# Transfers of the image preparation spread over twelve steps, and activation tables loaded in steps of their own

## The chip, the core and the metric

The kernel runs on one core of a Trainium2 chip. The metric is the device time of one execution in microseconds; the figure for a kernel is the median of several runs. The engines of the core run side by side, each through its own list of instructions in order: TensorE (PE in the profile, with its weight loads as PEld), VectorE (DVE), ScalarE (ACT), GpSimd (POOL) and SyncE (SP), which here does little but issue transfers (DMAs). They wait for each other by semaphores.

## What is computed

Four layers work on an image x of 4 batches, 32x32 pixels and 16 channels, each of the form x + layer(group_norm(x)). Layers 0, 1 and 3 are the heavy ones: every output pixel has a 3x3 convolution kernel of its own, whose result over the whole image is compared with the image and summed with weights. Layer 2 is a small dynamic program with two steps of sums, a sigmoid and a maximum. Cut to what matters:

```
def conv_layer(inputs, M, W, G):           # layers 0, 1 and 3 (inputs are normalized)
    first   = einsum('ijyx,byxc->bijc', M, inputs)
    kern    = transpose(G, (0, 1, 5, 4, 2, 3)).reshape(h * w * f, c, 3, 3)
    shifted = conv(x_nchw, kern, 'SAME')   # one 3x3 kernel per output pixel and channel
    diff    = relu(inputs[:, None, None] - shifted)
    second  = einsum('ijyx,bijyxc->bijc', W, diff)
    return first - second

def dp_step(f, r, W, b):                   # layer 2, twice
    g = sigmoid(ft[:, :, :, None, :] + rt[:, None, :, :, :] + b)
    return max(g, axis=2)

def _gn(v):                                # before every layer
    return (g - mean) / sqrt(var + eps)    # over 8 groups of channels
```

## The kernel before

**Phases and steps.** The batches are taken in two groups g of two. A phase is one heavy layer for one group; there are six, in the order (group 0, layer 0), (1, 0), (0, 1), (1, 1), (0, 2), (1, 2), where layer 2 in this count is the reference's layer 3. A phase has eight chunks of 128 output pixels, and a chunk 32 steps, one for each output channel and batch. A step fills one pair of PSUM banks (tile pc) with the convolution result for 128 output pixels against 1024 image pixels. There are 256 steps in a phase and 1536 in all, which this text numbers from 0.

In a step, `conv_layer` does this, in order: `first_part` issues eight matmuls of TensorE (L584, weights WU and WL against images iy and iz) and ScalarE's scaling of the result (L614); `second_part` of the step before issues six more matmuls (the weights WD and W9 against iyz and im9, into the scaled tile) and VectorE's weighted sum of the negative part (L630, tile junk). So TensorE needs L614 of a step one step later.

**Preparation of weights.** Four output channels (eight steps) form a unit. `prep_parts` prepares a unit's weights two units ahead, in eight pieces, one per step, which this text letters A to H: A, VectorE cuts off the upper bits (L191); B, ScalarE halves W9 (L167); C, ScalarE L224 and GpSimd L225 and L226; D, ScalarE L228 and GpSimd L229; E, GpSimd subtracts columns of the identity from the next unit's raw weights (L202); F, nothing; G, SP issues two transfers that copy parts with its halves exchanged (L235, 384 KB each), and the load of raw weights two units on (L107, 768 KB); H, nothing. The copy of a unit is seven steps ahead of its first use. Each piece tells with its yield whether the step is IDLE, that is, whether ScalarE has no such work in it: A, E, F, G and H are.

**Work behind the steps.** All else is written as generators (`behind`), which are resumed after a step's own instructions. They yield a number (so many steps until they go on) or IDLE (go on in the next idle step). In every phase but the last, `before_conv` prepares the images for the next one. `group_norm` takes sums on VectorE, with several small reductions `gap` steps apart (`totals`, used for the mean and then for the variance), the root on ScalarE (L324, then DVE's reciprocal L326 and the product on POOL L327). Then VectorE transposes the normalized image (L341), SP writes it to DRAM as xs with four transfers (L346), and two steps later SP begins the 24 transfers that read it back shifted, one for each of 12 (slot, row, tap) and each half h (L356, 68 KB each). They go out six per step over four steps, and after a pause of 24 or 12 steps the image tiles are made from raw (`split`, L259 and L263, `halve` and `difference`). As phase 0 takes its images directly, there are five such preparations, for phases 1 to 5.

Before layer 2, `interval_layer` runs behind phases 3 and 4. Its `step` does a DP step: eight times POOL adds a table (L541) and VectorE takes a maximum (L548), six steps apart; then ScalarE takes the sigmoid (L552), and SP writes the result back with four transfers.

**Activation tables.** ScalarE evaluates the root and the sigmoid from tables of which one set is held at a time; copies and scalings work with either. The program loads a set (ACT_TABLE_LOAD) ahead of an instruction that needs another than the last. It does so for the root at the start (L786), for the first sigmoid of each interval layer (L552), and for the next root after it (L324): five loads.

**Queue of SP.** L107, L113 (512 KB of the weights of the sum, once in a chunk), L235, L346 and L356 are all issued by SP, in program order, each after its own waits. Eight semaphores serve these transfers in turn, so each also waits until the eighth before it has landed.

Of the kernel before, what the change touches and what calls it, by code (L numbers as in the profile page):

```python
# [8 lines left out]
F32 = mybir.dt.float32  # L9
F32R = mybir.dt.float32r  # L10
I32 = mybir.dt.int32
AF = mybir.ActivationFunctionType
# [25 lines left out]
QI = H // NQ  # L38
# [3 lines left out]
def net_kernel(ctx: ExitStack, tc: tile.TileContext, x, xq, xi, convs, iv_w, iv_b, out):  # L42
# [26 lines left out]
    nc = tc.nc  # L69
    ctx.enter_context(tc.manual_schedule())  # L70

    const = ctx.enter_context(tc.tile_pool(name="const", bufs=1))
# [22 lines left out]
    IDLE = 0  # L95
# [49 lines left out]
    load_plain(nc.sync, 1, 0, FU)  # L145


    eps = const.tile([P, 1], F32, name="eps")
    nc.vector.memset(eps, 1e-5)
    ident = const.tile([P, P], F32, name="ident")  # L150
# [15 lines left out]
    def halve(dst, src, mask):  # L166
        nc.scalar.activation(dst, src, AF.Copy, scale=mask[:, 1:2])  # L167

    def halve_rest(dst, src, mask):
        nc.vector.scalar_tensor_tensor(  # L170
            dst, src, mask[:, 0:1], dst.bitcast(F32), op0=ALU.mult, op1=ALU.add
        )
# [11 lines left out]
    def image(v, x):  # L184
        return v.rearrange("... (y x) -> ... y x", x=x)[..., :H]
# [68 lines left out]
    def split(eng, g, b, name, pause=IDLE):  # L254

        high = upper(image(raw[:, :2, b], HP), 2, f"x{name}{b}")
        yield 1
        for s in range(2):
            eng.tensor_tensor(  # L259
                image(iz[g][:, s, b], H), image(raw[:, s, b], HP), image(high[:, s], H), ALU.subtract  # L260
            )
            yield pause
            nc.scalar.activation(iy[g][:, s, b], high[:, s], AF.Copy, scale=EPS)  # L263

    def difference(eng, g, b, s):
        eng.tensor_tensor(
            iyz[g][:, s, b], iy[g].bitcast(F32)[:, s, b], iz[g].bitcast(F32)[:, s, b],
            ALU.subtract,
        )
# [4 lines left out]
    def spread(stat):  # L274
        return stat.unsqueeze(1).unsqueeze(3).to_broadcast([P, NT, GC // 2, 2])

    def pair_view(ap):
        return ap.rearrange("p t (g s) -> p t g s", s=2)

    def group_norm(g, name, dst, gap):  # L280


        def sums(src):
            nc.vector.tensor_reduce(
                part[:, : GC // 2], src.rearrange("p t (g s) -> p g t s", s=2), axis=AX.XY, op=ALU.add
            )

        def totals(name):

            turned = work.tile([P, 32], F32, tag="turned", name=f"turned_{name}")  # L290
            nc.vector.transpose(turned, part)
            by_quarter = work.tile([32, 4], F32, tag="by_quarter", name=f"by_quarter_{name}")
            for q in range(4):
                nc.vector.tensor_reduce(
                    by_quarter[:, q : q + 1], turned[32 * q : 32 * q + 32], axis=AX.X, op=ALU.add
                )
            yield gap
            total = work.tile([P, 32], F32, tag="total", name=f"total_{name}")
            for q in range(4):
                nc.vector.tensor_reduce(  # L300
                    total[32 * q : 32 * q + 32, 0:1], by_quarter, axis=AX.X, op=ALU.add
                )
            yield gap
            whole = work.tile([P, 32], F32, tag="whole", name=f"whole_{name}")
            nc.vector.transpose(whole, total[:, 0:1].to_broadcast([P, 32]))
            return whole[:, : GC // 2]

        sums(X[g])
        yield gap
        m = yield from totals(f"m{name}")  # L310
        mean = work.tile([P, GC // 2], F32, tag="mean", name=f"mean_{name}")
        nc.gpsimd.tensor_scalar_mul(mean, m, 1.0 / (2 * NP))
        xc = work.tile([P, NT, GC], F32, tag="xc", name=f"xc_{name}")
        nc.gpsimd.tensor_tensor(pair_view(xc), pair_view(X[g]), spread(mean), ALU.subtract)
        sq = work.tile([P, NT, GC], F32, tag="sq", name=f"sq_{name}")
        nc.gpsimd.tensor_tensor(sq, xc, xc, ALU.mult)
        yield 4
        sums(sq)
        yield gap
        v = yield from totals(f"v{name}")  # L320
        yield 2
        yield IDLE
        rstd = work.tile([P, GC // 2], F32, tag="rstd", name=f"rstd_{name}")
        nc.scalar.activation(rstd, v, AF.Sqrt, bias=eps, scale=1.0 / (2 * NP))  # L324
        yield 2
        nc.vector.reciprocal(rstd, rstd)  # L326
        nc.gpsimd.tensor_tensor(pair_view(dst), pair_view(xc), spread(rstd), ALU.mult)  # L327
        yield 3
# [5 lines left out]
    def before_conv(g, layer):  # L334
        xn = work.tile([P, NT, GC], F32, tag="xn", bufs=2, name=f"xn_{g}_{layer}")
        xns[g] = xn
        yield from group_norm(g, f"c{g}{layer}", xn, 1 if layer == 2 else 4)

        nc.vector.transpose(  # L341
            xt[g][:, :, 1 : 1 + H], xn
        )
        inner = xs[g][:, HP : HP + H * HP].rearrange("p (t r n) -> p r t n", r=ROWS, n=HP)
        for r in range(ROWS):
            nc.sync.dma_start(inner[:, r], xt[g][GC * r : GC * (r + 1)])  # L346
        yield 2
        xsv = xs[g].rearrange("(b c) n -> c b n", b=GB)
        at = 0
        for slot, row, tap in [(tap // 4, tap % 4, tap) for tap in range(8)] + [  # L350
            (2, row, 8) for row in range(4)
        ]:
            for h in range(2):
                off = (HI * h + tap // 3) * HP + tap % 3
                r0 = 64 * h + C * row
                nc.sync.dma_start(  # L356
                    raw[r0 : r0 + C, slot ^ h if slot < 2 else 2, :, :RUN], xsv[:, :, off : off + RUN]
                )
            at += 1
            if at % 3 == 0:  # L360
                yield 1
        yield 12 if layer == 2 else 24
        for b in range(GB):
            yield from split(nc.gpsimd, g, b, f"{g}{layer}")
            yield IDLE
            halve(image(im9[g][:, b], H), image(raw[:, 2, b], HP), low_x)
            for s in range(2):
                difference(nc.gpsimd, g, b, s)
            yield 3
            halve_rest(image(im9[g][:, b], H), image(raw[:, 2, b], HP), low_x)  # L370
            yield 1
# [73 lines left out]
    def interval_layer(g):  # L445
# [85 lines left out]
        def step(name, ftp, bias):  # L531

            ft = ivp.tile([P, QI, T1], F32, tag="ft", name=f"ft_{name}{g}")
            nc.scalar.copy(ft, ftp)
            yield 2
            s = ivp.tile([P, QI, T1], F32, tag="s", name=f"s_{name}{g}")
            last = None
            for i in range(QI + 1):
                if i < QI:
                    t = dp[i % 2]  # L540
                    nc.gpsimd.tensor_tensor(  # L541
                        t,
                        ft[:, i, :].unsqueeze(1).to_broadcast([P, T1, T1]),
                        rt,
                        ALU.add,
                    )
                if last is not None:
                    nc.vector.tensor_reduce(s[:, i - 1, :], last, axis=AX.X, op=ALU.max)  # L548
                last = t
                yield 6  # L550
            yield IDLE
            nc.scalar.activation(s, s, AF.Sigmoid, bias=bias)  # L552
            for q in range(NQ):
                nc.sync.dma_start(r[R:, QI * q : QI * (q + 1), :], s[GC * q : GC * (q + 1)])
            yield 4
# [125 lines left out]
    def behind(phase):  # L681
        g, layer = phases[phase]
        if phase == 0:
            yield from rest_of_start()
            nc.scalar.dma_start(X[1], x[1])
            zeros(1)
            yield 1
            yield from constants()
        if phase + 1 < len(phases):
            g1, layer1 = phases[phase + 1]  # L690
            if layer1 == 2:
                yield from interval_layer(g1)
            terms = g1 == NG - 1 and layer1 < NL - 1
            if terms:
                mt = load_first_terms(layer1)
            yield from before_conv(g1, layer1)
            if terms:
                yield from first_terms(layer1, mt)
        if phase == len(phases) - 1:
            mt = load_first_terms(layer)  # L700
            yield 24
            yield from first_terms(layer, mt)
            yield 4
            nc.sync.dma_start(out[1 - g], X[1 - g])
# [228 lines left out]
```

## Time and profile before

| | us |
|---|---|
| median of 3 runs | 2594.79 (2590.87 to 2596.59) |
| the profiled execution | 2596.11 |
| its span in the profile | 2594.4 |
| L630 on VectorE, 1536 times | 1879.3 busy, 1224 ns each |
| L614 on ScalarE, 1520 times | 1531.8 busy, 1008 ns each |
| L225, L226, L229 on POOL, 190 times each | 246 to 247 busy each, about 1300 ns each |
| ACT_TABLE_LOAD, 5 times | 1283 ns each |
| L107, L235, L356 to landing, median | 7.2, 5.0, 2.4 |

The span is the time from the first to the last instruction of the profiled execution; the device time has 1.7 us more. Busy times are of the engine named, and engines overlap. A line of the timeline gives the start, the duration, the engine, the line, the operation, the tiles and how many instructions were merged; in brackets is the engine's idle time ahead of it. SPq is the sequencer of SP, where issuing a transfer takes its time. In the list of waits a line reads: who waited, for whom, the sum, how often and the longest.

### The profile page before, as it was taken

Reading aid. Unit: us, or ns where it says so; the run is one execution under the profiler, and the core shown is the slowest. Engines: PE = TensorE matmul, PEld = TensorE weight load, DVE = VectorE, ACT = ScalarE, POOL = GpSimd, SP = SyncE. Lnnn points to the kernel's source line nnn. Section 1 sums busy time; section 2 is a strip of 40 time slices with the busy share of each in tenths; the row PEclk is TensorE's granted clock in tenths of the full one; section 3 lists DMA queues with packets and bytes.
Section 4 is the critical chain, followed back from the end, with each engine's and each line's share of the span. In section 5 each row is a group of like instructions: output and inputs, shape, how many; then the busy total and the mean of one; then the engine's idle time right before and its main releaser. Section 6 shows DMA issues by size and latency. Waiting matters only on the chain.

```text
span 2594.4 us, 56655 instructions
## 1 busy us (share of the span) xinstructions
PE 2564.2 (99%) x21906; PEld 2158.5 (83%) x21906; DVE 2084.0 (80%) x3620; ACT 1893.7 (73%) x2169; POOL 1101.9 (42%) x990
## 2 busy tenths in 40 slices
PE   8999999999999999999999999999999999999999
PEld 5998888889888888888888887798888779788887
DVE  8887777878777877777788878788888878777777
ACT  4777677777777767777777777677777777677776
POOL 3444333444333435333345554354646344333332
PEclk9999999999999999999999999999999999999999
DMA  5655444464444653444444444544444466444442
GB/s 168 186 143 154 121 131 137 119 165 127 130 137 129 193 151 110 137 130 130 131 139 131 131 123 132 153 131 120 125 131 135 130 150 193 119 139 131 130 131 52
DMA packets 81182, 353.80 MB, mean 136 GB/s; under 512 B 18448, under 2 KB 20368, under 8 KB 80144
## 3 DMA queue, kind: packets, MB, share of 16 engines
q1 hardware_dynamic: 79920, 349.57, 48.1%
q8 instruction: 172, 2.82, 0.5%
q14 instruction: 98, 0.80, 0.1%
q10 hardware_dynamic: 864, 0.58, 0.1%
q0 software_dynamic: 128, 0.02, 0.0%
HBM read 199.19 MB, written 0.98 MB: 77 GB/s over the span
## 4 chain that ended last, share of the span: by engine, by line
PE 94%; DMA 2%; issue 1%; SPq 1%; DVE 0%; ACT 0%; POOL 0%; ACTq 0%; DVEq 0%; POOLq 0%
PE pc L584 93%; DMA parts<-parts 1%; PE pf L386 1%; SPq L356 1%; DMA raw<-in_g 0%; DMA raw<-in_xi 0%; ACT pc L614 0%; DVE junk L630 0%; DMA first<-in_g 0%; POOL parts L225 0%; PE ps_l L509 0%; SPq L346 0%; POOL W L226 0%; SPq L235 0%; PE ps_r L522 0%
## 5 line engine op out<-in xcount | busy, mean ns | idle before, releaser
L630 DVE SCALAR_TENSOR_TENSOR junk<-pc,WT 128x1024 f32<-128x1024 f32 x1536 | 1879.3, 1224 | 485.5 <-PE pc L584 440.1
L614 ACT ACTIVATE pc<-pc 128x1024 f32<-128x1024 f32 x1520 | 1531.8, 1008 | 665.1 <-PE pc L584 640.1
L584 PE MATMUL pc<-iy,parts 64*128 64x512 f32 x6080 | 1074.4, 394 | 13.5 <-DMA parts<-parts 13.5
L584 PE MATMUL pc<-iyz,parts 64*128 64x512 f32 x6080 | 1070.8, 394 | 4.0 <-ACT pc L614 4.0
L584 PE MATMUL pc<-iz,parts 64*128 64x512 f32 x6080 | 1070.6, 393 | 0.0
L584 PEld LDWEIGHTS pc<-iy,parts 64*128 64x128 f32 x6080 | 681.0, 185 | 129.0 <-DMA parts<-parts 17.0
L584 PEld LDWEIGHTS pc<-iz,parts 64*128 64x128 f32 x6080 | 681.5, 185 | 109.3
L584 PEld LDWEIGHTS pc<-iyz,parts 64*128 64x128 f32 x6080 | 660.3, 185 | 100.1 <-ACT pc L614 3.9
L584 PE MATMUL pc<-im,W 64*128 64x512 f32 x3072 | 725.4, 397 | 0.0
L225 POOL TENSOR_TENSOR parts<-raw,upper_w 128x512 fp32r<-128x512 f32 x190 | 246.1, 1295 | 1065.9 <-PE pc L584 923.7
L584 PEld LDWEIGHTS pc<-im,W 64*128 64x128 f32 x3072 | 382.7, 185 | 57.9 <-issue 3.4
L226 POOL TENSOR_TENSOR W<-W,raw 128x512 fp32r<-128x512 f32 x190 | 246.7, 1298 | 4.6 <-ACT W L167 4.6
L229 POOL TENSOR_TENSOR parts<-parts 128x512 fp32r<-128x512 f32 x190 | 246.7, 1298 | 2.0 <-ACT parts L224 1.6
L202 POOL TENSOR_TENSOR raw<-raw,ident 128x512 f32<-128x512 f32 x190 | 200.8, 1057 | 67.3 <-DMA raw<-in_g 67.3
L167 ACT ACTIVATE W<-raw,low_w 128x512 fp32r<-128x512 f32 x190 | 136.2, 717 | 0.1
L630 DVE DVE_READ_ACCUMULATOR junk<-pc,WT 128x1 f32 x1536 | 126.9, 83 | 0.0
L224 ACT ACTIVATE parts<-upper_w 128x512 fp32r<-128x512 f32 x190 | 118.5, 623 | 4.2 <-DVE upper_w L191 4.2
L228 ACT CAST parts<-upper_w 128x512 fp32r<-128x512 f32 x190 | 116.6, 614 | 0.0
L645 POOL TENSOR_SCALAR acc<-acc 128x32 f32<-128x32 f32 x40 | 11.5, 288 | 170.5 <-DVE junk L630 166.0
L191 DVE TENSOR_SCALAR upper_w<-raw 128x512 int32<-128x512 int32 x190 | 80.9, 426 | 0.0
L541 POOL TENSOR_TENSOR tables<-ft_b,rt 128x1089 f32<-128x1089 f32 x16 | 37.6, 2351 | 0.4 <-DVE s_b L548 0.4
L541 POOL TENSOR_TENSOR tables<-ft_a,rt 128x1089 f32<-128x1089 f32 x16 | 37.7, 2354 | 0.0
(137 smaller groups left out, 398.4 us busy)
## 6 DMA issues: line engine op xcount, KB each, us to landing
raw<-in_g SPq DMA_DIRECT2D x190, 768.0 KB, 7.2
parts<-parts SPq DMA_DIRECT2D x380, 384.0 KB, 5.0
WT<-in_w SPq DMA_DIRECT2D x48, 512.0 KB, 4.4
MT<-in_mt SPq DMA_DIRECT2D x6, 2048.0 KB, 13.4
raw<-xs SPq DMA_DIRECT2D x120, 67.8 KB, 2.4
raw<-in_xi SPq DMA_DIRECT2D x3, 271.0 KB, 4.7
raw<-in_xi SPq DMA_DIRECT2D x1, 813.0 KB, 7.7
xs<-xt SPq DMA_DIRECT2D x20, 34.0 KB, 2.4
```

The costliest lines, as they stand in the source:

```text
L167: nc.scalar.activation(dst, src, AF.Copy, scale=mask[:, 1:2])
L191: nc.vector.tensor_scalar(t.bitcast(I32), src.bitcast(I32), HIGH, None, op0=ALU.bitwise_and)
L202: eng.tensor_tensor(raws[u][:, s, at:to], raws[u][:, s, at:to], pick[s][:, f0 + at : f0 + to].unsqueeze(2).to_broadcast([P, to - at, P]), ...
L224: nc.scalar.activation(WD, high, AF.Copy, scale=-EPS)
L225: nc.gpsimd.tensor_tensor(WL, w8, high, ALU.subtract)
L226: nc.gpsimd.tensor_tensor(W9, W9.bitcast(F32), src[:, 2], ALU.add)
L228: nc.scalar.copy(WU, high)
L229: nc.gpsimd.tensor_tensor(WD, WD.bitcast(F32), WL.bitcast(F32), ALU.add)
L541: nc.gpsimd.tensor_tensor(t, ft[:, i, :].unsqueeze(1).to_broadcast([P, T1, T1]), rt, ALU.add,)
L584: nc.tensor.matmul(ps[:, h, :], lhsT=w[r], rhs=v[r], start=first and k == 0, stop=k == len(pairs) - 1, skip_group_check=not first,)
L614: nc.scalar.activation(ps, ps, AF.Copy, scale=1.0 + EPS)
L630: nc.vector.scalar_tensor_tensor(junk, ps.rearrange("p h n -> p (h n)"), 0.0, chunks[n], op0=ALU.min, op1=ALU.mult, accum_out=accs[phase][ ...
```

## The change

Three things are changed. The 24 transfers L356 go out two per step over twelve steps, in place of six per step over four, and the pause after them is 12 steps (6 in layer 2) in place of 24 (12). In `group_norm`, between the sums of the squares and the totals of the variance, the generator waits for an idle step and issues a root of a tile of one element, `spare`; in `step` of the interval layer it does the same with a sigmoid ahead of the real one, with the last of the nine pauses cut from six steps to three. POOL clears `spare` at the start.

```diff
+    spare = const.tile([1, 1], F32, name="spare")
+    nc.gpsimd.memset(spare, 0.0)
...
         yield 4
         sums(sq)
         yield gap
+        yield IDLE
+        nc.scalar.activation(spare, spare, AF.Sqrt)
         v = yield from totals(f"v{name}")
         yield 2
         yield IDLE
...
         xsv = xs[g].rearrange("(b c) n -> c b n", b=GB)
-        at = 0
         for slot, row, tap in [(tap // 4, tap % 4, tap) for tap in range(8)] + [
...
                 nc.sync.dma_start(
                     raw[r0 : r0 + C, slot ^ h if slot < 2 else 2, :, :RUN], xsv[:, :, off : off + RUN]
                 )
-            at += 1
-            if at % 3 == 0:
-                yield 1
-        yield 12 if layer == 2 else 24
+            yield 1
+        yield 6 if layer == 2 else 12
         for b in range(GB):
             yield from split(nc.gpsimd, g, b, f"{g}{layer}")
...
                 last = t
-                yield 6
+                yield 6 if i < QI else 3
+            yield IDLE
+            nc.scalar.activation(spare, spare, AF.Sigmoid)
+            yield 2
             yield IDLE
             nc.scalar.activation(s, s, AF.Sigmoid, bias=bias)
```

## The prediction

> **What bounds the kernel now.** I read the page first (shares of the engines), then TensorE's waits, then the busy time by stretch, then the DMA queue's and ScalarE's timelines at the places that these named.
>
> The page, and TensorE's waits (us in total, times, longest us):
>
> ```profile
> PE 2564.2 (99%) x21906; PEld 2158.5 (83%) x21906; DVE 2084.0 (80%) x3620; ACT 1893.7 (73%) x2169; POOL 1101.9 (42%) x990
> ```
>
> ```profile
> PE pc L584 <- DMA parts<-parts: 13.5, 8, 3.0
> ...
> PE pc L584 <- ACT pc L614: 4.0, 6, 1.0
> ```
>
> TensorE is busy 99% of the span, so only what makes it stop or run slowly can be won. It stops for the copies of parts (L235) in eight gaps, and for ScalarE's scaling of a PSUM tile (L614) in six small ones. By the chain of waits the eight gaps lie at five places: 201, 527, 946, 1673 and 2105 us, each just after the 24 transfers L356 of a `before_conv`. These gaps are not the whole loss. Busy time by stretch (us, then each engine's busy time and instructions, granted clock, DMA):
>
> ```profile
> 190.00:220.00 30.00, 27.03 (x217) 22.97 (x215) 19.50 (x34) 18.86 (x22) 9.65 (x8) 0.94 0.69 175
> 220.00:250.00 30.00, 30.00 (x262) 26.10 (x259) 23.62 (x40) 23.81 (x28) 15.16 (x14) 1.00 0.52 147
> 515.00:545.00 30.00, 28.98 (x245) 24.98 (x244) 22.07 (x37) 20.82 (x24) 9.65 (x8) 1.00 0.79 199
> 935.00:965.00 30.00, 27.40 (x209) 22.52 (x207) 19.01 (x32) 17.93 (x22) 9.65 (x8) 0.89 0.65 167
> 1660.00:1690.00 30.00, 26.83 (x205) 21.15 (x203) 18.87 (x32) 17.42 (x21) 10.15 (x10) 0.89 0.64 171
> 2095.00:2125.00 30.00, 26.27 (x211) 21.19 (x209) 19.31 (x34) 18.75 (x22) 13.45 (x13) 0.94 0.70 170
> ```
>
> The reader is to compare the first x, the matmuls begun. A quiet 30 us (220 to 250) begins 262; the five bad ones 217, 245, 209, 205 and 211, short by 223 in all. At 30/262 = 0.1145 us each that is 25.5 us, almost twice the 13.5 us of gaps. The clock column tells why: in four of the five it drops below 1.00 (0.57 from 204.2 to 208.2 us, 0.56 from 949.6 to 956.4), that is, after a long gap TensorE runs at half speed for a while. Taken step by step (start of one step's im matmuls to the next, 1.635 us when undisturbed) the excess is 4.9, 1.5, 6.0, 6.4 and 5.7: 24.5 us, which I use.
>
> Why the copies are late: the DMA queue of SP around the fourth place.
>
> ```profile
> 1649.97 1.81 SPq L346 DMA_DIRECT2D xs<-xt  x4
> 1651.95 1.11 SPq L235 DMA_DIRECT2D parts<-parts  x2
> 1653.11 1.23 SPq L107 DMA_DIRECT2D raw<-in_g  x1
> 1654.53 15.47 SPq L356 DMA_DIRECT2D raw<-xs  x24
> 1670.16 1.11 SPq L235 DMA_DIRECT2D parts<-parts  x2
> ```
>
> SP issues in order. 24 transfers at 0.467 us (18 took 8.23 to 8.24 at the first two places) would be 11.2 us; here they took 15.47, since the eighth after a weight load L107 waits for that load (the program gives the queue eight semaphores in turn). The copy behind them left at 1670.16, though L229 had finished its operands at 1657.1. TensorE ran dry before it landed.
>
> ScalarE around 1639 us, the table load for the root:
>
> ```profile
> 1638.18 1.01 ACT L614 ACTIVATE pc<-pc 128x1024 f32<-128x1024 f32 x1 [0.63 <-PE pc L584]
> 1639.21 1.28 ACT L324 ACT_TABLE_LOAD   x1
> 1640.50 0.31 ACT L324 ACTIVATE rstd_c<-whole_vc,eps 128x16 f32<-128x16 f32 x1
> 1640.72 0.71 ACT L167 ACTIVATE W<-raw,low_w 128x512 fp32r<-128x512 f32 x1
> 1641.33 1.00 ACT L614 ACTIVATE pc<-pc 128x1024 f32<-128x1024 f32 x1
> ```
>
> Load, root and the W9 halving stand between two L614; TensorE wanted the second at 1641.40 and got it at 1642.39.
>
> **What the Trainium skill says.** "TensorE: Matmul & The Clock Gate", Part 1, has two clock states, full and half, the half one after an idle window and back to full after about 3.4 us of work; the trace agrees (0.56 to 0.57 in windows just after gaps of 2 to 3 us, 1.00 throughout after the gap of 1.0 at 527). "DMA: Bandwidth & Descriptors", Queues, rings and completion order, says that descriptors on one engine's ring are consumed in ring order; the trace agrees in kind: small L356 transfers behind a load wait with it. "ScalarE: Activation LUTs", What ACT_TABLE_LOAD costs, gives 1283 ns plus a drain of 1380; the trace has the 1283 exactly, but the next ACTIVATE starts 0.01 us later, so I take no drain. The same section prices an ACTIVATE without pointer operands at 186 ns plus 0.833 per element, used below.
>
> **The change part by part.**
>
> *Spreading.* SP does not know steps; it issues as far as its waits let it. What counts is how many L356 now stand ahead of each copy L235 on its queue. Counting yields (the copy of a unit stands in the seventh of its eight steps, its first use seven steps on; the copies stay where they were): in the first, fourth and fifth preparation 6 stand ahead of the first copy, 16 between it and the second, 2 behind that; in the second and third, where the new idle step moves the whole chain by three steps, L346 stands just ahead of the first copy with no L356, then 16, then 8. Before it was 18 and 6 (three times) and 24 (twice).
> First preparation, with before's times: L356 can begin at 187.95 as now; 6 x 0.467 = 2.8, so the first copy goes at 190.8 instead of 196.34. With the slowest landing of the trace (196.34 to 203.95, 7.6 us) it is there at 198.4; TensorE ran dry at 201.0: 2.6 to spare. Its weight load starts at 192.0. At the fourth place load plus first 16 L356 took 13.1 us (1653.11 to 1670.00, less 8 x 0.467), the wait for the load included. So the second copy goes at 205.1, lands 6.4 later (1670.16 to 1676.6) at 211.5, and is needed 8 steps after the first, 201.0 + 13.1 = 214.1: 2.6 to spare. The fourth and fifth are alike.
> Second preparation: L346 is in step 295, which begins 9 x 1.635 = 14.7 us before the dry moment 527.1. L341 ended 2.75 us into its step in the first preparation (184.15, step begun at 201.0 - 12 x 1.635), L346 takes 1.85: the copy goes at 517.0, lands by 524.6, 2.5 to spare; load at 518.2, 16 transfers to 531.3, second copy in by 537.8, needed at 540.2: 2.4 to spare. So all five stalls go, with their slow clock: minus 24.5. Next late would be that second copy, from 2.4 us on.
> The shorter pause after the transfers (12 and 6 steps) is enough: the split needs the first 16 transfers (taps 0 to 7), which land some six steps or more before it. In layer 2 the second image is finished 8 steps later than before, in step 1020 for a first use in 1025: five steps, 8 us, cover it.
>
> *Tables.* The four loads move with a 1x1 ACTIVATE to an idle step. It costs between 0.19 us (the skill's price) and 0.26 (L786, 128x2 with a pointer bias, 263 ns); 0.22 taken. The load itself is not hidden: L614 leaves 0.63 us idle in a step and, undisturbed, would here have ended at 1638.18 + 1.635 + 1.01 = 1640.83, 0.57 before TensorE wanted it; 1.28 is more than the two. For the root: load to 1640.50, spare, L614 from 1640.70 to 1641.70 instead of 1642.33. The gap shrinks from 0.99 to 0.35; with 0.25 for restarting (the step's excess was 1.25 for a gap of 0.99) 0.65 is saved. For the sigmoid (1497.80 load, 0.52 for the sigmoid, gap 0.66) only 0.52 - 0.22 = 0.3 is saved. Two of each: minus 1.9 (from 0 if each load keeps its stall to minus 4.3 if idle steps took it whole). The real root, 0.30 in an idle step, already ran without loss at 96.2, and the sigmoid of the second DP step without load likewise.
>
> *The rest at nothing.* Eight other spare ACTIVATEs of 0.22 lie in idle steps with 0.63 free; if not, 1.8 in all. The memset of spare (0.10 to 0.12, as the others on POOL) delays ident; DVE then still waits 0.8 for raw<-in_xi, which hides it; otherwise plus 0.1. The last yield of the DP step is 3 instead of 6: the second sigmoid and its four transfers still move from step 951 to 954, and what follows by three steps; TensorE does not wait for it.
>
> Sum: 24.5 + 1.9 = 26.4. The profiled execution took 2596.1 (span 2594.4), so 2569.7; from the median of 2594.8, which is 1.3 below it, 2568.4. I take 2569.
>
> **Rivals.**
> - *One more copy late.* The second copy has only 2.4 to 2.6 us by my pessimistic landings. If bursts behind the load are slower by 3 to 4 us, it stalls by about 1 us in each place, which cost 1.5 at 527: up to 7.5, time 2573 to 2577. For it: the L356 next to a load took 1.4 to 2.0 instead of 0.42. Against: 24 of them with two such waits took 16.4 at most.
> - *Only the gaps are won.* If the slow clock had another cause than the gaps, 13.5 and the tables' 1.9 would go: 2581. Against: after the start it is absent everywhere else.
> - *Slower.* The same second copy, so late that each of five stalls exceeds 2 us and brings the half clock: at 6.5 each, like the third and fourth place, 32.5 are added to the 26.4 won: 2601. It decides when load plus 16 transfers takes over 18.5 us instead of 13.1; 24 took less.
> - *It doesn't do what it says.* "Two per step" does not pace SP, but the count between copies falls to 16 all the same; and the built program has its table loads at the spare ACTIVATEs.
>
> **How the numbers follow.** Likeliest 0.70; a copy late in some places 0.20; gaps only 0.04; slower 0.03; a loss I have not seen that eats the gain 0.03. A measurement can tell about 0.2% (5 us) from no change. Faster 0.94, same 0.03, slower 0.03. The likeliest alone spans 2565 to 2573 (tables 0 to 4.3, runs differing by 2); with the late copy the range is 2564 to 2579.
>
> **What would show it.** TensorE's wait for parts vanishes from its list; the five stretches have about 260 matmuls per 30 us and a clock of 1.00; L235 is preceded by at most 16 L356; two steps with a table load each keep gaps of 0.3 to 0.4. A wait for parts or for DVE's upper_x after a burst of 16 would make it wrong.

## The result and the profile after

The changed kernel takes 2568.84 us, the median of 4 runs (2568.38 to 2568.99), beside 2592.83 for the kernel before (2587.95 to 2596.59): a ratio of 0.9908 (95% interval 0.9890 to 0.9926). The prediction was 2569. The span of the profiled execution went from 2594.4 to 2566.6 us. In what follows the line numbers of the changed kernel are used for it: L237 is the copy of parts (before L235), L350 writes xs (L346), L359 reads it back (L356), L588 are the matmuls (L584), L618 the scaling (L614).

TensorE's waits after, all of them:

```profile
PE ps_own L766 <- DVE s L764: 4.8, 1, 4.8
PE pc L588 <- DVE raw L805: 2.0, 1, 2.0
PE pc L588 <- ACT pc L618: 1.7, 6, 0.4
PE ps_v L758 <- DVE by_batch_v L757: 1.4, 1, 1.4
```

The wait for parts, 13.5 us before, is gone from the list; that for the scaling fell from 4.0 to 1.7. The other three belong to the start. Busy time by stretch, at the five places (the last two are moved, as the program reaches them earlier) and in the quiet stretch between:

```profile
190.00:220.00 30.00, 30.00 (x262) 27.47 (x260) 23.81 (x40) 22.20 (x26) 10.57 (x9) 1.00 0.74 203
220.00:250.00 30.00, 30.00 (x262) 27.16 (x262) 26.05 (x44) 26.59 (x33) 24.29 (x22) 1.00 0.44 124
515.00:545.00 30.00, 30.00 (x260) 24.22 (x258) 23.06 (x41) 23.19 (x27) 13.33 (x12) 1.00 0.72 190
935.00:965.00 30.00, 30.00 (x262) 24.19 (x260) 23.12 (x39) 22.70 (x26) 11.61 (x10) 1.00 0.70 189
1650.00:1680.00 30.00, 30.00 (x260) 23.83 (x256) 24.32 (x41) 23.22 (x28) 14.55 (x14) 1.00 0.85 211
2075.00:2105.00 30.00, 30.00 (x259) 23.95 (x256) 24.32 (x41) 23.21 (x29) 14.75 (x14) 1.00 0.86 218
```

The matmuls begun in 30 us are 259 to 262 in all five, where 205 to 245 were before, and the clock column reads 1.00 throughout: with the gaps the slow stretches behind them are gone too.

The queue of SP at the fourth place:

```profile
1641.74 2.66 SPq L350 DMA_DIRECT2D xs<-xt  x4
1647.29 2.67 SPq L359 DMA_DIRECT2D raw<-xs  x6
1650.06 1.11 SPq L237 DMA_DIRECT2D parts<-parts  x2
1651.21 1.24 SPq L107 DMA_DIRECT2D raw<-in_g  x1
1652.49 11.57 SPq L359 DMA_DIRECT2D raw<-xs  x16
1664.22 1.10 SPq L237 DMA_DIRECT2D parts<-parts  x2
```

The reader is to see two things. The transfers still go out in one run as fast as the queue lets them, not two per step of 1.63 us; and a copy now stands behind 6 and behind 16 of them, where one stood behind 24.

ScalarE at the load for the root:

```profile
1622.52 1.01 ACT L618 ACTIVATE pc<-pc 128x1024 f32<-128x1024 f32 x1 [0.63 <-PE pc L588]
1623.55 1.28 ACT L323 ACT_TABLE_LOAD   x1
1624.84 0.20 ACT L323 ACTIVATE spare<-spare 1x1 f32<-1x1 f32 x1
1624.95 1.00 ACT L618 ACTIVATE pc<-pc 128x1024 f32<-128x1024 f32 x1
```

The root and the halving of W9 no longer stand between two scalings. The load still does, and TensorE still waits 0.26 us there (1625.74 to 1626.00).

Taken step by step as in the prediction (1.633 us for an undisturbed step), the excess of the profiled executions, in us:

| place | before | after |
|---|---|---|
| five places behind L356 | 4.9, 1.5, 6.0, 6.4, 5.7 | 0 |
| two loads for the sigmoid | 0.90, 0.90 | 0.52, 0.52 |
| two loads for the root | 1.25, 1.26 | 0.52, 0.52 |
| small excesses in steps of the image preparation | 0.07 in five steps | 0.16 to 0.23 in four steps |

24.5 and 2.2 us are gained, 0.4 lost (at 1678 us, for one, ScalarE has L265 of the preparation and the halving of W9, L169, between two scalings). Of the remaining 1.5 of the 27.8 us between the spans, 1.1 is the start: step 16 begins at 45.4 instead of 46.5 us. It began at 46.4 in another execution of the changed kernel, so this is chance and not the change. The last 0.4 is spread over other steps.

### The profile page after: what moved, and what is told of

Its sections match the earlier page's. It is cut to its first block, busy times and chain, and to the rows that moved or that the text cites. A ratio compares the mean times of both kernels' runs of the same rounds, so it can differ in the third digit from the quotient of the medians.

```text
span 2566.6 us, 56663 instructions
## 1 busy us (share of the span) xinstructions
PE 2552.4 (99%) x21906; PEld 2064.8 (80%) x21906; DVE 2079.7 (81%) x3620; ACT 1894.8 (74%) x2181; POOL 1102.1 (43%) x991
## 4 chain that ended last, share of the span: by engine, by line
PE 99%; ACT 0%; DVE 0%; issue 0%; POOL 0%; DVEq 0%; ACTq 0%; POOLq 0%
PE pc L588 98%; PE pf L387 1%; ACT pc L618 0%; PE ps_l L510 0%; PE ps_r L523 0%; DVE junk L634 0%; ACT L323 0%; DVE raw L805 0%; PE ps_y L574 0%; DVE kept L748 0%; ACT L553 0%; PE ps_v L758 0%; DVE raw L813 0%; DVE kept L744 0%; DVE squares L781 0%
## 5 line engine op out<-in xcount | busy, mean ns | idle before, releaser
L618 ACT ACTIVATE pc<-pc 128x1024 f32<-128x1024 f32 x1520 | 1531.8, 1008 | 637.2 <-PE pc L588 607.4
L588 PE MATMUL pc<-iyz,parts 64*128 64x512 f32 x6080 | 966.5, 393 | 1.7 <-ACT pc L618 1.7
L588 PE MATMUL pc<-iy,parts 64*128 64x512 f32 x6080 | 967.8, 393 | 0.0
L588 PE MATMUL pc<-iz,parts 64*128 64x512 f32 x6080 | 965.3, 392 | 0.0
L588 PEld LDWEIGHTS pc<-iyz,parts 64*128 64x128 f32 x6080 | 583.0, 185 | 133.8 <-ACT pc L618 5.5
L588 PEld LDWEIGHTS pc<-iy,parts 64*128 64x128 f32 x6080 | 582.3, 185 | 132.5 <-issue 4.4
L588 PEld LDWEIGHTS pc<-iz,parts 64*128 64x128 f32 x6080 | 584.0, 185 | 128.6
L588 PE MATMUL pc<-im,W 64*128 64x512 f32 x3072 | 622.6, 396 | 0.0
L588 PEld LDWEIGHTS pc<-im,W 64*128 64x128 f32 x3072 | 295.4, 185 | 68.6 <-issue 3.5
L169 ACT ACTIVATE W<-raw,low_w 128x512 fp32r<-128x512 f32 x190 | 136.1, 716 | 0.1
```

The lines of the kernel that those rows point to most:

```text
L588: nc.tensor.matmul(ps[:, h, :], lhsT=w[r], rhs=v[r], start=first and k == 0, stop=k == len(pairs) - 1, skip_group_check=not first,)
L618: nc.scalar.activation(ps, ps, AF.Copy, scale=1.0 + EPS)
```

## The experiments

Seven more kernels were run, and the changed one once more. All times are medians; the kernel before is 2591 to 2594 beside them. The table has those that are about the copies.

| kernel | transfers per step | what stands ahead of the copies | TensorE's waits for parts | time |
|---|---|---|---|---|
| before | 6 | 18, 6 and 24 | 13.5 us | 2592.83 |
| changed | 2 | 6, 16, 2 and 0, 16, 8 | none | 2568.84 |
| e1_spread | 2 | 6, 16, 2 and 0, 14, 10 | none | 2570.45 |
| e2_tables | 6 | 18, 6 and 24 | 10.1 us | 2585.95 |
| e3_12_12 | 6 | 12, 12 and 0, 12, 12 | 0.6 us | 2569.42 |
| e4_24 | 24 | 0, 24 | 3.7 us | 2573.42 |
| e5_ahead | 24 (three of five places) | 24 | 15.6 us | 2592.66 |

**The two halves alone.** The question was whether the spreading itself frees the copies, or the shift of three or four steps that the spare ACTIVATEs bring to the preparation. First the spreading without spare:

```diff
-    spare = const.tile([1, 1], F32, name="spare")
-    nc.gpsimd.memset(spare, 0.0)
...
-        yield IDLE
-        nc.scalar.activation(spare, spare, AF.Sqrt)
...
-                yield 6 if i < QI else 3
-            yield IDLE
-            nc.scalar.activation(spare, spare, AF.Sigmoid)
-            yield 2
+                yield 6
```

> The changed kernel without spare and its ACTIVATEs (the pause in the DP step back at six): only the transfers are spread. My theory (the copies L235 no longer wait behind more than 16 transfers): no wait of TensorE for parts is left, and the four table loads keep their steps of 0.9 and 1.25 us, so some 2.2 us above the changed kernel: 2571. Rival (the shift of the preparation by three or four steps, which the spare instructions bring, is what frees the copies): waits for parts stay in two to four places, 2578 to 2590.

Measured: 2570.45 us (2570.10 to 2571.05), with no wait for parts, and ScalarE's wait back at its old size:

```profile
PE pc L581 <- ACT pc L611: 4.0, 6, 1.0
```

The spreading alone wins the copies. The steps with a load have an excess of 0.91, 1.25, 0.91 and 1.26 again, 2.2 us more than in the changed kernel. On the other side it has none of the small excesses of the image preparation, 0.8 us in the changed kernel; in the medians the difference is 1.6. So spare wins at the loads and loses some of it by the shift that it brings.

Then spare on the kernel before, with its six transfers per step:

> The kernel before with the spare ACTIVATEs alone, the transfers still six per step. My theory: all five places still stall, since 18 or 24 transfers stand in one stretch ahead of a copy, and only 2.2 us are saved at the table loads: 2588 to 2595, not to be told from before. Rival (the shift frees the copies): 2570 to 2580.

Measured: 2585.95 us (2581.49 to 2587.95), ratio 0.9967 (0.9958 to 0.9975) to the kernel before: lower than I expected. All five places still stall, with 5.8, 0.8, 2.0, 6.3 and 2.4 us of step time: less in sum, though the first, where the order on the queue is as before, costs more. In the second place the shift puts the copy ahead of the transfers instead of behind 18 of them:

```profile
515.91 1.81 SPq L350 DMA_DIRECT2D xs<-xt  x4
517.88 1.11 SPq L237 DMA_DIRECT2D parts<-parts  x2
519.03 1.24 SPq L107 DMA_DIRECT2D raw<-in_g  x1
520.51 15.05 SPq L360 DMA_DIRECT2D raw<-xs  x24
535.73 1.11 SPq L237 DMA_DIRECT2D parts<-parts  x2
```

All 24 then stand ahead of the next copy, which is late by less (a gap of 0.6 instead of 1.0 us). So the shift has a part of its own, some 7 us of step time in the profiled executions. It is not all order: 1.7 us of gap at the third place and 1.9 at the fifth brought no half clock here, which the last section explains. Once the transfers are spread the shift takes no wait for parts away, as e1_spread shows.

**Rate or place.** If what counts is the number of transfers between two copies on the queue, six per step must do as well in the right place.

```diff
+        pause = {3: 1, 6: 7, 9: 1} if layer == 1 else {3: 1, 6: 2, 9: 1}
...
+            if k in pause:
+                yield pause[k]
             for h in range(2):
...
-            yield 1
-        yield 6 if layer == 2 else 12
+        yield (18 if layer == 2 else 24) - sum(pause.values())
```

> The changed kernel, but the transfers go out six per step over four steps as before, two of these steps ahead of a copy of parts and two behind it, so that 12 stand on each side. My theory (what counts is how many stand ahead of a copy on the queue of SP, not how many a step issues): within 3 us of the changed kernel, 2568 to 2572. Rival (six per step are too many whatever their place): the five stalls come back, 2585 to 2597.

Measured: 2569.42 us (2568.78 to 2572.06), a median within the 2568.4 to 2570.0 that the changed kernel took over all its runs, with a single wait for parts of 0.6 us. At the fourth place:

```profile
1649.08 5.46 SPq L362 DMA_DIRECT2D raw<-xs  x12
1654.70 1.11 SPq L237 DMA_DIRECT2D parts<-parts  x2
1655.85 1.39 SPq L107 DMA_DIRECT2D raw<-in_g  x1
1657.29 9.96 SPq L362 DMA_DIRECT2D raw<-xs  x12
```

Twelve transfers go out in 5.46 us, 0.455 us each, and six took 2.67 us, 0.445 each, in the changed kernel with its two per step: the rate in the program is not what paces the queue. The next kernel puts all 24 into one step, just behind a copy (pause = {} for layer 1, {0: 3} otherwise):

> The changed kernel, but all 24 transfers go out in one step, the one whose copy of parts has just been issued, so that all 24 stand between two copies and as early as they can. My theory: the queue takes some 17 us for load and 24 transfers; in the first, fourth and fifth preparation they begin early enough for the next copy (no stall), in the second and third the copy comes 4 us later than in the changed kernel and misses its use by about 1 us, 1.5 us of time each: 2570 to 2576. Rival (the number in one step decides): worse than before, over 2595.

Measured: 2573.42 us (2571.56 to 2577.56; the profiled execution is the slowest of the four). The first, fourth and fifth place have no stall, the second and third have one. There the gaps were 2.3 and 1.5 us, a little over the 1 expected, but the cost was 4.1 and 3.5 us of step time instead of 1.5, since 3.4 us at half clock came with each (lines in the last section).

Last the other end: all 24 in one step too, but ahead of the first copy, in the first, fourth and fifth place (pause = {} there; in layer 1 one step before each pair but the first, as in the changed kernel):

> The changed kernel, but in the first, fourth and fifth preparation all 24 transfers go out in one step two steps after xs, so that all 24 stand ahead of the first copy of parts; the second and third stay as in the changed kernel. The number of transfers per step is the same as in the kernel with all 24 behind a copy (2573.4 us); only the place differs. My theory: 24 transfers take 11.2 us from the landing of xs, the copy leaves at about 198 instead of 189.6 us and lands 4 to 6 us after TensorE ran dry, the half clock follows; 6 to 9 us each, three times: 2587 to 2596. Rival (the place does not matter): about 2573.

Measured: 2592.66 us (2590.99 to 2594.27). Three stalls of 6.3, 8.6 and 7.8 us of step time give back all that the change won. The first of them:

```profile
183.47 1.82 SPq L350 DMA_DIRECT2D xs<-xt  x4
187.14 11.02 SPq L362 DMA_DIRECT2D raw<-xs  x24
198.33 2.49 SPq L237 DMA_DIRECT2D parts<-parts  x2
```

The copy left at 198.33, where the changed kernel's left at 189.56, and TensorE stood from 199.96 to 203.38.

**What a table load still costs.** 0.52 us of step time is left at each of the four. First ScalarE was relieved of one scaling in the step after each load (`loads` gets an entry at each of the four ACTIVATEs of spare that load a table):

```diff
+        if gap == 1:
+            loads.append(name)
...
+            if name == "a":
+                loads.append(name)
...
-        nc.scalar.activation(ps, ps, AF.Copy, scale=1.0 + EPS)
+        if loads:
+            loads.clear()
+            nc.vector.tensor_scalar_mul(ps, ps, 1.0 + EPS)
+        else:
+            nc.scalar.activation(ps, ps, AF.Copy, scale=1.0 + EPS)
```

> The changed kernel, but in the step after each of the four table loads VectorE instead of ScalarE scales the PSUM tile (one of L618's instructions each). My theory: the load of 1.28 us is more than ScalarE's idle time and so still holds TensorE by 0.52 us of step time; with the scaling taken away it fits, VectorE has room for 1.1 us within a few steps: 2.1 us less than the changed kernel, 2566.5 to 2567.5. Rival (VectorE becomes late and TensorE waits for its tiles instead): 2568.5 or more.

Measured: 2571.3 us (2570.22 to 2571.5), slower than the changed kernel: the rival was right. VectorE at the load for the root:

```profile
1624.67 0.21 DVE L293 STREAM_TRANSPOSE turned_vc<-part 128x32 f32<-128x32 f32 x1
1624.91 0.74 DVE L296 TENSOR_REDUCE by_quarter_vc<-turned_vc 32x1 f32<-32x32 f32 x4
1625.69 0.43 DVE L193 TENSOR_SCALAR upper_w<-raw 128x512 int32<-128x512 int32 x1
1626.03 1.23 DVE L624 TENSOR_SCALAR pc<-pc 128x1024 f32<-128x1024 f32 x1
```

The totals, which follow the spare root in the program, and upper_w stand ahead of the scaling, and TensorE waits 1.3 us for it at both roots (excess 1.6 instead of 0.52). At the sigmoids, where VectorE had no totals, the excess was 0.49 and 0.23.

Then three of the four loads were taken away, with the root worked out by instructions that need no table (the changed kernel was run once more beside it):

```diff
-        nc.scalar.activation(spare, spare, AF.Sqrt)
...
-        nc.scalar.activation(rstd, v, AF.Sqrt, bias=eps, scale=1.0 / (2 * NP))
...
+        nc.vector.tensor_scalar(var, v, 1.0 / (2 * NP), 1e-5, op0=ALU.mult, op1=ALU.add)
...
+        for turn in range(3):
+            nc.gpsimd.tensor_tensor(near, rstd, rstd, ALU.mult)
+            nc.gpsimd.tensor_tensor(near, near, var, ALU.mult)
+            nc.gpsimd.tensor_scalar(near, near, -0.5, 1.5, op0=ALU.mult, op1=ALU.add)
+            nc.gpsimd.tensor_tensor(rstd, rstd, near, ALU.mult)
         yield 2
-        nc.vector.reciprocal(rstd, rstd)
```

> The changed kernel once more, beside the next one on the same chip: 2568 to 2570.

> The changed kernel with the inverse root of group_norm worked out without a table (three VectorE instructions on 128x16 and twelve of POOL in place of ScalarE's root, of spare's root and of the reciprocal; all steps stay where they are; the root at the start stays). Only the first interval layer's sigmoid still loads a table, three of the four loads are gone. My theory: each load left in the changed kernel costs 0.52 us of step time, so 1.6 us less than the changed kernel on the same chip: 2566.5 to 2568. Rival (the load is hidden already, or POOL's 3 us delay a unit's weights): the same time or more.

Measured: 2568.25 us (2568.15 to 2569.09) beside 2569.30 (2568.89 to 2569.96). This is 1.05 us less, not 1.6, and the ranges touch. In the profile the three excesses of 0.52 are gone, and one new wait is there:

```profile
PE pc L599 <- ACT pc L629: 0.9, 3, 0.4
PE pc L599 <- DMA parts<-parts: 0.4, 1, 0.4
```

It lies at 2148.7 us, behind the two 2 MB loads of MT, where the copy had come in 0.9 us ahead of its use in the changed kernel, and costs 0.64 of step time; why the copy was late there stays open. So 1.57 are won and 0.64 lost. This version has the lowest median of those run, by a margin that is hardly more than the spread.

## Why the prediction was right

- *The number.* The sum, 26.4 off the profiled 2596.1, gives 2569.7; the profiled execution after took 2568.4, 1.1 of the difference being the chance start. That 2569 agrees with the median to 0.2 us is luck. Between the medians 24.0 us were won; 26.4 off the median before, 2592.83, would have given 2566.4, still in the range. The profiled execution before took longer than that median, as the stalls cost more in some executions than in others (last section).
- *What the five stalls cost.* The prediction took 24.5 us, gaps and half clock together, and in the profiled executions all of it was won. The rival of the gaps alone (2581) fails: the clock is 1.00 at all five places.
- *Which part of the change wins it.* It said that SP isn't paced by steps and that the count ahead of each copy decides. e3_12_12 (six per step, 2569.4), e4_24 (24 in a step, 2573.4) and e5_ahead (24 in a step ahead of the copy, 2592.7) show this. A faster flight of the copies, with fewer transfers beside them, is not what did it: by the semaphores in the traces the five late ones took 5.6 to 7.6 us from leaving to landing, and the copies of the same five units 5.5 to 6.1 in the changed kernel. What moved is their leaving, 5.4 to 7.9 us earlier against their use.
- *The room of the copies.* 2.4 to 2.6 us were worked out. At the first place the copy left at 189.56 (190.8 predicted) and the second at 203.05 (205.1), and by the traces they landed 4.3 and 3.9 us before their use: more room than predicted. The 7.6 us called the slowest landing was not that (the copy of 2106.89 took 12.1, one of 119.76 took 13.5), but the first two copies at each place landed in 5.5 to 6.9. "The fourth and fifth are alike" was wrong: there the first transfer left 5.55 us after L350 began (1641.74 to 1647.29), not 3.8, everything behind it came later, and the second copy landed only some 1.4 us before its use. It still sufficed, and the rival of one more copy late stayed out; e3_12_12, with twelve ahead of each copy, ran dry for 0.6 us at the second copy of the fifth place.
- *Tables.* 1.9 predicted, 2.2 at the loads in the profiled executions, 1.6 between the medians with and without spare, as the shift costs some of it. The spare ACTIVATE took 0.185 to 0.202 us for 0.22 assumed, and the gap was 0.26 for 0.35. That the load itself is not hidden held.
- *The slower case.* It priced a stall with half clock at 6.5 us each; the three of e5_ahead cost 6.3 to 8.6. The mechanism is real. In the changed kernel the second copies of the fourth and fifth place are 1.4 us away from a gap, and the half clock begins later still.
- *Edits at nothing.* The eight other spare ACTIVATEs have no step with an excess; the memset of spare and the later second sigmoid cost nothing that can be seen. The shift of the image preparation cost 0.4 us more than its place before, which was not in the sum.

## What to carry to other kernels

A queue that issues in order knows nothing of the steps in the program: count what stands ahead of each urgent transfer, and when the first of it may leave, rather than how many a step issues. A stall of TensorE can cost more than its gap; compare instructions begun per stretch with a quiet stretch, look at the granted clock, and take several executions, since the same gap may bring the half clock in one and not in another. A table load placed in an idle step is hidden only as far as that step and the slack behind it reach; what is moved out of its way, the instructions after it, is the gain.

## What the runs showed of the hardware that was not expected

The half clock does not follow from the length of the gap alone. In e4_24 gaps of 2.3 and 1.5 us were each followed by 3.4 us at half clock; in the kernel before, 1.0 us at 527 was followed by none; in e2_tables, 1.7 us at 960, and 0.5 and 1.4 us close together at 2100, were followed by none either. "TensorE: Matmul & The Clock Gate" of the Trainium skill, Part 1, calls the window free-running, so that a gap's place in it would matter, and the clock records of the ten traces show it. Within each execution the granted clock changes only at times that lie whole multiples of 3.413 us apart, wherever the gaps are, and this grid starts elsewhere in each execution. Cut along it, the third places of e4_24 (two lines) and of e2_tables (three) read:

```profile
957.20:960.61 3.41, 1.95 (x15) 1.35 (x15) 1.16 (x2) 0.57 (x2) 0.00 (x0) 1.00 0.97 200
960.61:964.02 3.41, 3.41 (x20) 2.61 (x18) 1.23 (x2) 1.63 (x2) 0.00 (x0) 0.50 1.01 234
956.98:960.40 3.42, 2.88 (x25) 2.44 (x22) 2.62 (x5) 2.24 (x3) 0.00 (x1) 1.00 0.98 224
960.40:963.81 3.41, 2.24 (x20) 1.86 (x22) 0.94 (x3) 1.01 (x1) 0.00 (x0) 1.00 0.99 259
963.81:967.22 3.41, 3.41 (x32) 3.14 (x31) 2.61 (x5) 2.02 (x2) 1.04 (x1) 1.00 1.02 220
```

The reader is to take PE's busy time, the third figure, from the length of the window, and to read the clock of the next window, the third figure from the end. In e4_24 TensorE was idle for 1.46 us within one window, and the next has the clock 0.50. In e2_tables a longer gap was cut in two by the border, 0.54 and 1.17 us, and both windows behind it have 1.00. So it is over all ten traces, though the ends of matmuls are modelled and the idle times approximate: of 7483 windows at full clock, the 21 with 1.46 us or more of idle time were each followed by one at half clock, and none of the 7462 others, with 1.42 or less, was. Of the 17 at half clock, the six with 0.80 us or more were followed by another, the eleven with 0.41 or less by a full one. No window need be idle throughout: in the first line TensorE worked for more than half of it.

The stalls also made the spread. The kernel before ranged from 2587.6 to 2598.3 us over its runs, the changed one from 2568.4 to 2570.0. Over 39 runs of the kernel before, each with its mean granted clock on record, the seven at 0.995 took 2597.0 us on the mean and the seven at 0.998 took 2589.1. In the main, the longer an execution took, the more of it ran at half clock. And the four sets of runs without a wait for parts (the changed kernel twice, e1_spread, e6_dve_scale) range over at most 1.3 us, those with 3.7 us of it or more (before, e2_tables, e4_24, e5_ahead) over 3.3 to 10.8.
